# A four-layer graph network on one core: the negative part of layer 1's activation in half-size buffers

## The chip, the cores and the metric

The kernel runs on one core of a Trainium2 chip. The metric is the device time of that core in microseconds. The kernel before takes 2318.61 us, the median of three runs (2318.61 to 2320.24). One further execution was recorded by the hardware profiler; its own time was 2319.3 us, and its span, from the first to the last instruction, is 2317.5 us.

## The reference, cut to what matters

A stack of four graph layers is applied to 32 independent tiles. A tile is `x` (512 tokens of 256 features) with its own 512 x 512 matrix `adj`, all float32. Each layer multiplies by `adj`, by small weight matrices, adds `x` back and normalizes every token (`ln`, a layer norm without weights). Layer 1, where the change lies, has one weight and a leaky activation with slope `alpha`:

```
# layer 0: x = ln(x + relu(((1 + eps) * x + adj @ x) @ W1 + b1) @ W2 + b2)
# layer 1:
h = seq @ W.T + b
h = adj @ h
x = ln(x + where(h > 0, h, alpha * h))
# layer 2: a layer norm first, then x + relu(adj @ h @ W_rel + b_rel + h @ W_root), then ln
# layer 3: epsilon * x + adj @ x, a dense layer of 1024, an rms norm, silu, a dense layer back to 256, ln
```

## The kernel before, in words

**Tiles and layers.** The 512 tokens of a tile lie as 4 chunks of 128 (NC = 4) over the 128 partitions; a half of the tokens is two chunks (HC = 2). `layer0` to `layer3` list the operations of one tile, in a loop over the 32 tiles (`plan.graph` is the tile's number). The products with `adj` and most dense products use seven block products in place of eight (`seven`), which costs VectorE the sums of blocks (`right_sums`, `left_sums`) and the additions that put the products together (`put`).

**Layer 1's end.** For each half of the tokens, `dense_tok` leaves W times the aggregate in PSUM; VectorE writes `v` = b * (row sum) + that, chunk by chunk. Then ScalarE writes `neg` = relu(-v) for the half (`act`, line 1072), VectorE does x = x - alpha * neg (`stt` with `nalpha`, line 1073) and then v = max(v, 0) + x (line 1074). `Norm.half` adds up v on ScalarE. After both halves the tile's `h`, `xx` and, with one `stt` for each chunk, `u` (the bias terms of layer 2) follow.

**An order written by a planner.** None of these calls issues anything. They record operations, and `Plan.order` places all 16956 of them with a list scheduler of its own: each engine in turn takes, of the operations that could start at the earliest moment, the one with the lowest rank. The rank of an operation is its tile's number times 42, plus how much TensorE work of its tile stands before the work that needs it; the last three tiles (LATE = 3) are spaced by the third number of a rule in place of 42. `best` (line 348) works out the order for every rule in `RULES` (line 95) and keeps the one whose last operation starts first by the planner's own table of durations. Of the two rules, that is the first, with 10. The order of the instructions on the engines in the trace is this rule's. The program then issues the operations in that order on five engines; waits between engines are semaphores.

**Rooms.** SBUF buffers are placed by the same planner. There are 36 tiles of 1024 floats for each partition (`rooms`), each made of two halves. A value that covers all tokens (`tok()`, `room()`) takes a whole one; a value of half the size (`short()`) takes a half. A room is taken when the planner places the first operation that uses it, and is free again after the last. `rooms_free` decides whether an operation may take its rooms:

```
if not r.whole and k < len(halves):
    taken[pool, False] = k + 1
    at = max(at, halves[k][0])
    continue
...
n += pool.spare[min(op.graph - oldest, len(pool.spare) - 1)]
if n >= len(whole):
    return None
```

So an operation that takes a whole room must leave a reserve of whole rooms that grows with how far its tile is ahead of the oldest unfinished one: none, 2, 4, and 4 for tiles three and more ahead (`spare` on line 526). An operation that takes a half has no such duty while a half stands free beside an occupied one; only if there is none must it break a whole room under the same reserve. Where both exist, `Pool.take` (line 127) breaks a whole room instead if one has been free for more than 1 us longer than the half. At most five tiles are in work at once (FLIGHT = 5). Halves are otherwise used by the block sums of the dense layers (`dense_sums`, three at a time), by the row sums, and by two values of layer 3.

Of the kernel before, what the change touches and what calls it, by code (L numbers as in the profile page):

```python
# [11 lines left out]
AF = mybir.ActivationFunctionType  # L12
ALU = mybir.AluOpType
# [7 lines left out]
def span(ap):  # L21

    n = 1
    for d in ap.shape[1:]:
        n *= d
    return n
# [65 lines left out]

RULES = [(42, 2, 10, 0.5), (42, 2, 16, 0.5)]


class Pool:
# [122 lines left out]
class Plan:  # L221
# [126 lines left out]
    def best(self):  # L348


        rule = min(RULES, key=lambda rule: self.order(*rule)[0])
        return self.order(*rule)[1]
# [109 lines left out]
def tile_gnn_stack(ctx: ExitStack, tc: tile.TileContext, a: dict, out: bass.AP):  # L462
# [26 lines left out]
    B, N, D = a["x"].shape  # L489
# [6 lines left out]
    HC = NC // 2  # L496
# [36 lines left out]
    def scalar(func, n, x, times=scalar_time, **kw):  # L533
        columns = sum(k in ("scale", "bias") and not isinstance(v, float) for k, v in kw.items())
        return "scalar", "activation", times(n, columns), (x,), dict(func=func, **kw)
# [9 lines left out]
    def act(o, x, func, **kw):  # L545
        plan.do(o, scalar(func, span(o), x, **kw))
# [20 lines left out]
    def stt(o, x, s, y, op0, op1):  # L567
        times = (vector_time if isinstance(s, float) else columns_time)(span(o))
        way = "vector", "scalar_tensor_tensor", times, (x, s, y), dict(op0=op0, op1=op1)
        plan.do(o, way)  # L570
# [11 lines left out]
    def room(*shape):  # L582
        return Part(Room(rooms)).shaped(*shape)

    def short(*shape):
        return Part(Room(rooms, whole=False)).shaped(*shape)

    def small(*shape):
        return Part(Room(smalls)).shaped(*shape)
# [4 lines left out]
    def tok():  # L594
        return room(NC, D)

    def half(t, h):
        return t[:, h * HC : (h + 1) * HC]
# [16 lines left out]
    def constant(name, shape):  # L615
        return const.tile(shape, F32, tag=name, name=name)
# [150 lines left out]
    def aggregate(x, adjacency):  # L767

        aT = room(DC, N)
        blocks = [  # L770
            x[:, j * HC : (j + 1) * HC, k * P : (k + 1) * P] for j in range(2) for k in range(2)
        ]
        t = room(4, HC, P)
        right = right_sums(*blocks, [t[:, i] for i in range(3)], t[:, 3])

        def product(m, ps, first):
            for k in range(HC):
                mm(ps, right[m][:, k, :], adjacency.left[m][:, k, :], first and k == 0, k == HC - 1)

        def block(i, k):  # L780
            return aT[:, k, i * TH : (i + 1) * TH]

        def take(ps, i, k):
            copy(block(i, k), ps)

        def put(ps, i, k, more):
            if more:
                add(block(i, k), ps, block(i, k))
            else:
                take(ps, i, k)  # L790

        seven(*(bank(TH) for _ in range(3)), product, take, put)
        return aT

    def dense_tok(steps, h):

        ps = bank(HC, D)
        for n, (xT, W) in enumerate(steps):
            for i in range(HC):
                c = h * HC + i  # L800
                mm(
                    ps[:, i, :], xT[:, c * P : (c + 1) * P], W,
                    n == 0 and i == 0, n == len(steps) - 1,
                )
        return ps
# [69 lines left out]
    def column_sums(t):  # L875

        few = small(N // Q)
        plan.do(  # L880
            few,
            (
                "vector", "tensor_reduce", vector_time(N), (t.shaped(N // Q, Q),),
                dict(axis=mybir.AxisListType.X, op=ALU.add, apply_transpose=True),
            ),
        )
        for q in range(1, P // Q):
            add(few[0:Q], few[0:Q], few[q * Q : (q + 1) * Q])
        return few[0:Q]

    def by_token(o, sums, *ops):

        for q in range(P // Q):
            ts(o[q * Q : (q + 1) * Q], sums[:, q :: P // Q], *ops)
# [141 lines left out]
    def load_x(b):  # L1036
        x = tok()
        src = a["x"][b].rearrange("(p c) d -> p c d", c=NC)
        if b:
            plan.move(x, src, N * D / 256, late=1.6)  # L1040
        else:
            for h in range(2):
                plan.move(half(x, h), half(src, h), N * D / 512, late=1.6)
        return x

    def layer0(x, adjacency):
        adjacency.sums()
        adjacency.with_loops(loop0)
        aT = aggregate(x, adjacency)
        adjacency.restore()  # L1050
        plus_row(x, b2_0)
        h1 = Wide(FC0)
        dense_feat(aT, A1_0, b1_0, h1, lambda f: act(h1.pair(f), h1.pair(f), AF.Relu))
        norm = Norm(x)
        dense_add(x, dense_sums(h1.rooms[:1], h1.rooms[1:]), A2_0, norm.half)
        norm.scales((1.0, LN_EPS))
        return norm.scaled()

    def layer1(x, adjacency):

        rows = adjacency.row_sums()
        aT = aggregate(x, adjacency)
        rs = small(NC)
        by_token(rs, column_sums(rows), 1.0, None, ALU.mult)
        v, neg = tok(), tok()
        norm = Norm(v)
        for h in range(2):
            ps = dense_tok([(aT[:, k, :], W_1[:, k, :]) for k in range(DC)], h)
            for i in range(HC):
                c = h * HC + i  # L1070
                stt(v[:, c, :], b_1, rs[:, c : c + 1], ps[:, i, :], ALU.mult, ALU.add)
            act(half(neg, h), half(v, h), AF.Relu, scale=-1.0)
            stt(half(x, h), half(neg, h), nalpha, half(x, h), ALU.mult, ALU.add)
            stt(half(v, h), half(v, h), 0.0, half(x, h), ALU.max, ALU.add)
            norm.half(h)

        norm.scales((1.0 + LN_EPS, LN_EPS * LN_EPS), (0.25, 0.25 * LN_EPS))
        h = norm.scaled(0)
        xx = norm.scaled(1)
        u = tok()  # L1080
        for c in range(NC):
            stt(u[:, c, :], shift_rel, rs[:, c : c + 1], shift_2, ALU.mult, ALU.add)
        return h, xx, u
# [68 lines left out]
    x = load_x(0)  # L1152
# [8 lines left out]
    nalpha = constant("nalpha", [P, 1])  # L1161
# [3 lines left out]
    x = layer0(x, adjacency)  # L1165
# [7 lines left out]
    add(shift_2, shift_2, b_2)  # L1173
    A_2 = weight_sums("A_2", *blocks_of(Wroot, Wrel))
    h = layer1(x, adjacency)
    W1_3 = weight("L3_gnn_W1")
    W2_3 = weight("L3_gnn_W2")
# [9 lines left out]
    for b in range(1, B):  # L1187
        plan.graph = b
        x, adjacency = load_x(b), Adjacency(b)
        h = layer1(layer0(x, adjacency), adjacency)  # L1190
        layer3(layer2(*h, adjacency), adjacency, b)
# [44 lines left out]
```

## Time and profile before

| what | value |
|---|---|
| median of three runs | 2318.61 us (2318.61 to 2320.24) |
| profiled execution, its own time | 2319.3 us |
| its span | 2317.5 us |
| TensorE matmul busy | 2295.5 us, 99% |
| TensorE weight load busy | 2089.9 us, 90% |
| VectorE busy | 2120.0 us, 91% |
| ScalarE busy | 1642.6 us, 71% |
| GpSimd busy | 256.9 us, 11% |
| granted TensorE clock | 0.999 |
| DMA, mean share of 16 engines | 19.1% for the data queue |

The span is that of the profiled execution; 1.8 us of its own time lie outside it. A group of the profile gives the engine, the operation, the result and its sources by buffer name, the shapes, the count, the busy time and the mean of one. Line 298 is the planner's `issue` helper, through which every planned operation goes, so groups are told apart by names and shapes: `room` is any of the 36 rooms, `few` the small vectors, `ps` a bank of PSUM.

### The profile page before, as it was taken

How to read it: one execution, taken by the hardware profiler on the slowest of the kernel's cores; microseconds unless marked ns; L12 is line 12 of the kernel's file. 1: busy time of each engine (PE TensorE's matmuls, PEld its weight loads, DVE VectorE, ACT ScalarE, POOL GpSimd, SP SyncE). 2: the span in 40 equal slices, each digit the busy share in tenths (PEclk: the TensorE clock that was granted, in tenths of full speed). 3: DMA queues.
4: the chain of work that ended last, by engine and by line, in shares of the span. 5: the costliest groups of instructions: out<-in, count | busy, mean ns of one | idle time of the engine just before them, and what ended most of it. 6: DMA issues, size and time to landing. Idle time of an engine off the chain costs nothing.

```text
span 2317.5 us, 41158 instructions
## 1 busy us (share of the span) xinstructions
PE 2295.5 (99%) x14002; PEld 2089.9 (90%) x14002; DVE 2120.0 (91%) x5428; ACT 1642.6 (71%) x4444; POOL 256.9 (11%) x167
## 2 busy tenths in 40 slices
PE   9999999999999999999999999999999999999998
PEld 7889899999999999999999999999999999998988
DVE  8989999999899999999999999989999899989897
ACT  4676677776776776777767776767677677676776
POOL 0000001101101101011011111010110101101110
PEclk9999999999999999999999999999999999999999
DMA  7001222112221122211222211222112222201101
GB/s 241 21 18 19 62 58 60 24 55 62 58 60 28 54 59 65 55 43 41 56 65 57 60 25 56 61 58 59 38 46 58 65 55 52 78 13 24 55 15 42
DMA packets 223746, 122.83 MB, mean 53 GB/s; under 512 B 142896, under 2 KB 194352, under 8 KB 223536
## 3 DMA queue, kind: packets, MB, share of 16 engines
q1 hardware_dynamic: 223536, 120.20, 19.1%
q8 instruction: 111, 1.82, 0.3%
q14 instruction: 99, 0.81, 0.1%
HBM read 78.92 MB, written 24.97 MB: 45 GB/s over the span
## 4 chain that ended last, share of the span: by engine, by line
PE 89%; DVE 7%; ACT 2%; DMA 1%; issue 1%; SPq 0%; POOL 0%; ACTq 0%; DVEq 0%
PE ps L298 89%; DVE room L298 6%; ACT room L298 1%; ACT scrap L298 1%; DVE few L298 1%; DMA room<-in_x_dram 1%; DMA L_gnn_W<-in_L_gnn_W_dram 0%; DMA room<-in_adj_dram 0%; DMA L_gnn_b<-in_L_gnn_b_dram 0%; DMA diagonal<-room 0%; SPq L316 0%; ACT L298 0%; DVE A L298 0%; DVE L_gnn_W_root L298 0%; POOL few L298 0%
## 5 line engine op out<-in xcount | busy, mean ns | idle before, releaser
L298 PE MATMUL ps<-room,room 128*128 128x256 f32 x3584 | 930.9, 381 | 5.7 <-DVE room L298 3.2
L298 DVE TENSOR_TENSOR room<-room,room 128x512 f32<-128x512 f32 (+1 forms) x1360 | 773.0, 590 | 5.4 <-ACT room L298 2.8
L298 DVE TENSOR_TENSOR room<-ps,room 128x256 f32<-128x256 f32 (+1 forms) x1344 | 605.6, 469 | 143.7 <-PE ps L298 136.4
L298 PEld LDWEIGHTS ps<-room,room 128*128 128x128 f32 x3584 | 617.3, 191 | 70.3 <-DVE room L298 7.1
L298 PE MATMUL ps<-L_gnn_W,room 128*128 128x128 f32 (+1 forms) x3584 | 544.3, 290 | 1.9 <-DVE room L298 1.0
L298 PEld LDWEIGHTS ps<-L_gnn_W,room 128*128 128x128 f32 x3584 | 505.6, 191 | 33.7 <-ACT room L298 1.9
L298 PEld LDWEIGHTS ps<-A,room 128*128 128x128 f32 x3072 | 460.5, 191 | 47.3 <-DVE room L298 14.1
L298 PE MATMUL ps<-A,room 128*128 128x128 f32 x3072 | 486.9, 276 | 0.9 <-DVE room L298 0.7
L298 POOL TENSOR_TENSOR few<-few,mhalf 128x4 f32<-128x4 f32 (+2 forms) x161 | 256.2, 1598 | 2054.5 <-DVE few L298 1883.1
L298 ACT ACTIVATE room<-room,few 128x256 f32<-128x256 f32 x627 | 335.0, 596 | 159.9 <-DVE few L298 159.7
L298 PE MATMUL ps<-room,L_gnn_W 128*128 128x256 f32 x1536 | 416.4, 380 | 0.6 <-DVE room L298 0.5
L298 ACT ACTIVATE room<-ps,L_gnn_b_c 128x256 f32<-128x256 f32 x768 | 311.0, 476 | 122.3 <-PE ps L298 117.9
L298 DVE TENSOR_TENSOR room<-room 128x256 f32<-128x256 f32 (+1 forms) x640 | 308.7, 492 | 13.9 <-ACT room L298 8.2
L298 PE MATMUL ps<-room,A 128*128 128x256 f32 x1152 | 320.0, 380 | 1.1 <-ACT room L298 0.8
L298 ACT ACTIVATE room<-room 128x1024 f32<-128x1024 f32 (+2 forms) x260 | 240.8, 939 | 87.3 <-DVE room L298 84.4
L298 PEld LDWEIGHTS ps<-room,L_gnn_W 128*128 128x128 f32 x1536 | 274.5, 191 | 30.1 <-DVE room L298 1.9
L298 ACT ACTIVATE room<-ps 128x256 f32<-128x256 f32 (+1 forms) x513 | 180.1, 373 | 153.3 <-PE ps L298 153.1
L298 ACT ACTIVATE scrap<-room,few 128x256 f32<-128x256 f32 x504 | 250.7, 499 | 39.0 <-DVE few L298 38.3
L298 ACT ACTIVATE scrap<-room 128x256 f32<-128x256 f32 x504 | 206.7, 411 | 88.3 <-DVE room L298 79.8
L298 PEld LDWEIGHTS ps<-room,A 128*128 128x128 f32 x1152 | 202.8, 191 | 22.8 <-ACT room L298 2.0
L298 ACT ACTIVATE room<-room,L_gnn_rms_weight_c 128x512 f32<-128x512 f32 x256 | 173.2, 712 | 13.1 <-DVE room L298 11.0
L298 DVE TENSOR_TENSOR room<-room,loop 128x256 f32<-128x256 f32 x256 | 101.1, 411 | 2.9 <-DMA diagonal<-room 1.8
(57 smaller groups left out, 1110.6 us busy)
## 6 DMA issues: line engine op xcount, KB each, us to landing
room<-in_adj_dram SPq DMA_DIRECT2D x128, 256.0 KB, 5.0
room<-in_x_dram SPq DMA_DIRECT2D x31, 512.0 KB, 5.9
out_dram<-room SPq DMA_DIRECT2D x31, 512.0 KB, 3.2
room<-room SPq DMA_DIRECT2D x480, 32.0 KB, 2.0
diagonal<-room SPq DMA_DIRECT2D x62, 128.0 KB, 1.8
room<-in_adj_dram SPq DMA_DIRECT2D x124, 64.0 KB, 1.9
room<-diagonal SPq DMA_DIRECT2D x62, 128.0 KB, 2.2
room<-line SPq DMA_DIRECT2D x30, 256.0 KB, 3.3
```

What stands on the lines that cost most here:

```text
L298: getattr(getattr(self.nc, engine), method)(to, *(put(x) for x in args), **kw)
```

## The change

`neg` is no longer one whole room that holds both halves of the tokens. In each pass of the loop over the halves a half room is asked for with `short(HC, D)`, used by the Relu and by the `stt` with `nalpha`, and given back. Beside it the second rule is taken out of `RULES`. The instructions of the program, their engines, shapes and number are the same.

```diff
-RULES = [(42, 2, 10, 0.5), (42, 2, 16, 0.5)]
+RULES = [(42, 2, 10, 0.5)]
...
-        v, neg = tok(), tok()
+        v = tok()
         norm = Norm(v)
         for h in range(2):
             ps = dense_tok([(aT[:, k, :], W_1[:, k, :]) for k in range(DC)], h)
             for i in range(HC):
                 c = h * HC + i
                 stt(v[:, c, :], b_1, rs[:, c : c + 1], ps[:, i, :], ALU.mult, ALU.add)
-            act(half(neg, h), half(v, h), AF.Relu, scale=-1.0)
-            stt(half(x, h), half(neg, h), nalpha, half(x, h), ALU.mult, ALU.add)
+            neg = short(HC, D)
+            act(neg, half(v, h), AF.Relu, scale=-1.0)
+            stt(half(x, h), neg, nalpha, half(x, h), ALU.mult, ALU.add)
             stt(half(v, h), half(v, h), 0.0, half(x, h), ALU.max, ALU.add)
             norm.half(h)
```

## The prediction

> **What bounds the kernel now.** I read the first part of the page, then the busy time in four stretches, then TensorE's waits, then the groups that the change touches. First the page: busy time, share of the span, instructions.
>
> ```profile
> PE 2295.5 (99%) x14002; PEld 2089.9 (90%) x14002; DVE 2120.0 (91%) x5428; ACT 1642.6 (71%) x4444; POOL 256.9 (11%) x167
> ```
>
> TensorE is the bound, VectorE is not far behind. A mean hides where the slack lies, so next the windows view: stretch, its length, then busy time of PE, PEld, DVE, ACT and POOL, clock, DMA share.
>
> ```profile
> 72.00:290.00 218.00, 213.22 (x1272) 190.78 (x1270) 201.96 (x522) 147.22 (x391) 19.80 (x14) 1.00 0.12 29
> 290.00:1955.00 1665.00, 1665.00 (x10191) 1521.11 (x10190) 1532.03 (x3896) 1207.55 (x3290) 194.14 (x118) 1.00 0.20 52
> 1955.00:2309.00 354.00, 351.13 (x2201) 321.27 (x2199) 318.88 (x814) 248.33 (x660) 37.83 (x25) 1.00 0.14 38
> 2309.00:2317.50 8.50, 0.00 (x0) 0.00 (x0) 2.86 (x13) 4.14 (x11) 1.72 (x3) 0.66 0.47 185
> ```
>
> For 1665 us TensorE never stands still. Its idle time lies at the edges: 5.88 us in the first 72 (the page of windows of 72 us gives 66.12 busy there), 218.00 - 213.22 = 4.78 us up to 290, 354.00 - 351.13 = 2.87 us in the tail, and 8.5 us after the last matmul. Who ends TensorE's waits from 2046 on, and from 55 to 290 (the waits view in each window: total, times, longest)?
>
> ```profile
> PE ps L298 <- DVE room L298: 2.2, 4, 1.1
> PE ps L298 <- ACT room L298: 0.2, 1, 0.2
> ...
> PE ps L298 <- DVE room L298: 3.5, 7, 1.5
> PE ps L298 <- ACT room L298: 1.5, 3, 0.7
> ```
>
> At both edges it is VectorE's results that come late, mostly. What the change touches are two groups (by form: count, busy, mean ns of one, idle before), and one tile's pair of them in the middle, from the timelines of ScalarE and VectorE (start, duration):
>
> ```profile
> L298 ACT ACTIVATE room<-room 128x512 f32<-128x512 f32 x64 | 39.8, 622 | 9.4 <-DVE room L298 7.8
> L298 DVE SCALAR_TENSOR_TENSOR room<-room,nalpha,room 128x512 f32<-128x512 f32 x64 | 47.1, 737 | 0.9 <-ACT room L298 0.9
> ```
>
> ```profile
> 1435.82 0.61 ACT L298 ACTIVATE room<-room 128x512 f32<-128x512 f32 x1
> 1438.09 0.63 ACT L298 ACTIVATE room<-room 128x512 f32<-128x512 f32 x1
> ```
>
> ```profile
> 1436.54 0.73 DVE L298 SCALAR_TENSOR_TENSOR room<-room,nalpha,room 128x512 f32<-128x512 f32 x1
> 1439.26 0.73 DVE L298 SCALAR_TENSOR_TENSOR room<-room,nalpha,room 128x512 f32<-128x512 f32 x1
> ```
>
> Each is 64 instructions, two a tile, already on half the tokens. The whole room of `neg` is held from 1435.82 to 1439.26 + 0.73 = 1439.99: 4.2 us of the 71.2 us that a tile takes (the same Relu stands at 1364.64 one tile before).
>
> **What the Trainium skill says.** "Perfetto Trace Analysis", Identifying the Most-Contended Engine, warns that matmul busy time does not tell how near TensorE is to its limit and asks for the busy share of the weight loads. Here that is 2089.9 / 2317.5 = 90%, and 1521.11 / 1665 = 91% in the middle; together with no wait at all in the middle, I take TensorE as full there. The same page, Optimization Strategy, says that a gap which repeats on the engine that should be full can mean that there is too little SBUF for the next tile. The trace shows no such gap between 290 and 1955, so space is not what limits the middle. "VectorE: DVE Perf Modes", on the TRN2 errata, puts a fixed cost on each instruction; more or larger instructions would thus cost something, but the change alters neither count nor size.
>
> **The change part by part.**
>
> *Instructions.* Removed 0, added 0. The Relu stays 128x512 (622 ns), the `stt` stays 128x512 (737 ns), no DMA moves with them: 64 x 0 = 0 us.
>
> *The second rule.* The plan before is the first rule's, which stays. Taking the other out changes nothing by itself; it only leaves the new plan with no alternative: 0 us.
>
> *The room.* A whole room for 4.2 us becomes a half for about 1.5 us (1435.82 to 1437.27) and a half for 1.9 us (1438.09 to 1439.99). This pays only where an operation waits for a room. I followed the kernel's own bookkeeping of rooms along the trace's order of instructions:
>
> In the middle (tiles 5 to 27) nine whole rooms and a half stand free when the Relu comes, eight whole after it. Nobody waits for a room in those 4.2 us, so nothing moves: 0 us for 23 tiles. If a wait did appear in each, it would be paid in full, since TensorE has no idle time to hide it.
>
> At the start, tile 0's Relu is at 54.45. Between its two halves, at 58.76, a block sum of another tile takes a half and breaks a whole room for it; now it can use the half beside `neg`, and one whole room more stays. The same happens at 160.58 inside tile 2's `neg` (159.19 to 162.52), with five whole rooms free and tile 3 waiting for one: its `u` write needs five and finds four. From there the order can shift until about 290.
>
> In the tail, tile 28's Relu comes at 2046.43 with five whole rooms and one half free. It is two tiles ahead of the oldest, so it must leave four, and takes the fifth. Tiles 29 and 30 wait to write `u`, need five as well, and get their rooms at 2054.06 and 2057.38. With the change `neg` uses the old half, five whole rooms stay, and tile 29's `u` may start some 7.6 us sooner. It is a value that is only needed in layer 2 (whose products begin for tile 29 at 2092.6), so it occupies a room sooner than it is of use. What is late next is not `neg` of the second half itself: tile 28's layer 2 begins on TensorE at 2087.6, about 34 us after the last step of its layer 1 (2053.13). It is the other takers of rooms, all of which come in another order for the last 263 us.
>
> The trace does not show the new order, so I bound its cost. Best: all idle time of the two affected stretches goes, -(4.78 + 2.87) = -7.65 us. Worst: the tail feeds TensorE as poorly as the stretch 72 to 217, where rooms are shortest: 4.31 us idle in 145 (the 72 us windows give 70.82 of 73 and 69.87 of 72), 2.97%. Over 2309 - 2046.4 = 262.6 us that is 7.8 us against 2.55 now (idle from 2046 on: 1.26 + 0.15 + 0.41 + 0.73), +5.25 us; and the start's 4.78 us double: together +10.0 us. I take the middle of -7.65 and +10.0, which is +1.2 us. Sum: 0 + 0 + 0 + 1.2: span 2317.5 to 2318.7, own time 2319.3 to 2320.5. The median of the runs stands 0.7 us below the profiled execution's own time, so 2319.8.
>
> **The rivals.** A difference of 0.2%, 4.6 us, is about what a measurement of this kernel can tell from none.
>
> *Same*, 2319.8 (2314.0 to 2323.2): the middle cannot move, the edges shift by a few us either way. For it: 1665 of 2317.5 us without a wait and with eight rooms to spare. A form of it is that the change does not do what it says for the time: only addresses of rooms differ and the order stays, 2318.6. Against that form: tile 28's Relu releases a taker at once.
>
> *Slower by the tail*, 2323.9: at 2046.43 the room that is saved goes to `u` of tile 29, rooms for the values that TensorE needs come later, and the tail runs at the start's supply: +5.25. It decides from 4.6 us more, that is 7.2 us idle in the last 263. For it: the whole rooms there fall to two, and VectorE, whose results end TensorE's waits, is 90% busy (318.88 of 354). Against: the shift is one room for 7.6 us.
>
> *Slower in the middle*, 2324.7: the weight loads wait 46 times for VectorE between 290 and 1955, 11.9 us in all, 0.26 us each, none of which stops a matmul today. If the new order let one such wait through for each tile, 1665 / 71.2 = 23.4 tiles give 6.1 us. It needs 0.2 us a tile. Against: no room is short there.
>
> *Faster*, 2313.5: two thirds of the 7.65 us go, -5.1, since rooms are what start and tail lack. For it: operations waiting for rooms at both places. Against: the idle time is VectorE's lateness, and its work does not shrink.
>
> **How the numbers follow.** Same 0.54. Slower 0.32: by the tail 0.24, in the middle 0.05, by the start alone 0.03. Faster 0.14. The tail is reordered as a whole with little idle to win and more to lose, hence slower over faster. The likeliest is same, 2319.8. For 8 in 10 the range goes from 2313.0, just below the faster case, to 2329.0, the worst sum (2318.6 + 10.0 = 2328.6); I leave out some 0.05 below and 0.10 above.
>
> **What would show it.** Right: 64 Relus and 64 `stt` with `nalpha` at 622 and 737 ns; TensorE busy for the whole of 290 to 1955; a repeat of 71.2 us; tile 29's `u` (VectorE, from `shift_rel`) between the two halves of tile 28; differences only before 290 and after 1955. Wrong: idle time of TensorE that repeats in the middle, or more than 7.2 us of it after 2046, or the 8.5 us after the last matmul grown, because another tile's end stands beside the last one's.

## The result, and the profile after

The changed kernel takes 2323.11 us (median of 20 runs, 2321.32 to 2325.10) against 2319.34 us of the kernel before in the same comparison (20 runs): ratio 1.0016, 95% interval 1.0009 to 1.0023. That is 3.77 us, or 0.16%: inside the 0.2% that the prediction called the same, inside its range, but at the upper end of the likeliest case (2323.2) and three times the 1.2 us of its sum. The profiled execution of the changed kernel took 2323.66 us with a span of 2321.9 us, 4.4 us more than before by either measure.

The first part of the page of the changed kernel:

```profile
PE 2297.9 (99%) x14002; PEld 2091.5 (90%) x14002; DVE 2119.8 (91%) x5410; ACT 1640.7 (71%) x4443; POOL 256.5 (11%) x167
```

VectorE has 18 instructions fewer than before (5410 for 5428) and ScalarE one fewer, so not every instruction stayed as it was: in its new order the planner sets 53 short pauses on VectorE (`memset` of `pause`, about 0.1 us each) where it was 72, and it gives three operations to the other one of VectorE and ScalarE. The two groups of the change are the same, by form:

```profile
L298 DVE SCALAR_TENSOR_TENSOR room<-room,nalpha,room 128x512 f32<-128x512 f32 x64 | 47.0, 735 | 2.0 <-ACT room L298 2.0
L298 ACT ACTIVATE room<-room 128x512 f32<-128x512 f32 x64 | 39.9, 623 | 9.3 <-DVE room L298 7.6
```

735 and 623 ns where it was 737 and 622: the time is not in these instructions. The windows view (stretch, length, busy time of PE, PEld, DVE, ACT, POOL, clock, DMA share, GB/s) shows the stretch that matters, the middle and the tail, first in the changed kernel:

```profile
150.00:175.00 25.00, 21.71 (x120) 18.84 (x119) 23.94 (x55) 18.40 (x48) 2.64 (x2) 0.93 0.04 12
290.00:1955.00 1665.00, 1664.94 (x10188) 1520.10 (x10188) 1531.22 (x3892) 1205.97 (x3287) 194.24 (x118) 1.00 0.20 52
2046.00:2309.00 263.00, 260.17 (x1635) 238.78 (x1633) 238.20 (x588) 186.79 (x499) 28.34 (x18) 1.00 0.10 24
```

then the first and the last of them in the kernel before:

```profile
150.00:175.00 25.00, 23.38 (x133) 19.97 (x132) 23.88 (x55) 20.73 (x54) 2.64 (x2) 1.00 0.04 12
2046.00:2309.00 263.00, 260.44 (x1645) 238.66 (x1643) 237.57 (x607) 191.60 (x512) 30.45 (x20) 1.00 0.10 26
```

In 25 us TensorE gets through 120 matmul records where it was 133 (a product stands as two records in these traces), with 1.67 us less busy time and a granted clock of 0.93. The middle is as full as it was, and the tail has 2.83 us of idle time against 2.56, far from the 7.2 us that the prediction named as a sign of being wrong. To put a number on each stretch I added up, over all successive products in a trace, the time from one start to the next beyond what a product takes when nothing waits (0.432 us at 256 columns, 0.223 us at 128), and took the time from the last product's end to the end of the span by itself:

| us lost on TensorE | before | after | difference |
|---|---|---|---|
| first product to 150 | 13.35 | 13.29 | -0.06 |
| 150 to 176 | 2.97 | 6.33 | +3.36 |
| 176 to 290 | 1.43 | 1.89 | +0.46 |
| 290 to 1955 | 10.04 | 10.40 | +0.36 |
| 1955 to 2046 | 1.54 | 1.23 | -0.31 |
| 2046 to the last product | 5.47 | 6.59 | +1.12 |
| after the last product | 8.57 | 7.97 | -0.60 |
| sum | 43.37 | 47.70 | +4.33 |

The difference of the sums is that of the two spans (2321.85 - 2317.52). Three quarters of it lie in 26 us. TensorE's timeline there (start, duration, what, idle before and who ended it), kernel before:

```profile
161.46 0.59 PE L298 MATMUL ps<-room,A 128*128 128x256 f32 x2
161.89 1.14 PE L298 MATMUL ps<-room,room 128*128 128x256 f32 x4
162.87 1.05 PE L298 MATMUL ps<-L_gnn_W,room 128*128 128x128 f32 x8
164.41 0.71 PE L298 MATMUL ps<-L_gnn_W,room 128*128 128x128 f32 x4 [0.49 <-DVE room L298]
164.96 1.03 PE L298 MATMUL ps<-room,room 128*128 128x256 f32 x4
```

and after:

```profile
161.39 0.59 PE L298 MATMUL ps<-room,A 128*128 128x256 f32 x2
161.82 1.05 PE L298 MATMUL ps<-L_gnn_W,room 128*128 128x128 f32 x8
162.71 1.03 PE L298 MATMUL ps<-room,A 128*128 128x256 f32 x4
164.35 1.16 PE L298 MATMUL ps<-L_gnn_W,room 128*128 128x128 f32 x8 [0.61 <-DVE room L298]
167.08 1.32 PE L298 MATMUL ps<-L_gnn_W,room 128*128 128x128 f32 x8 [1.57 <-ACT room L298]
168.79 1.12 PE L298 MATMUL ps<-A,room 128*128 128x128 f32 x4 [0.39 <-DVE room L298]
169.71 1.91 PE L298 MATMUL ps<-L_gnn_W,room 128*128 128x128 f32 x8
171.41 1.28 PE L298 MATMUL ps<-room,room 128*128 128x256 f32 x3
```

A product of `room` with `room` here is tile 1's layer-3 aggregate; those of `L_gnn_W` and `A` with `room` at 128 columns are tile 0's last dense layer. Before, the two take turns from 161.89 on, and tile 1 covers the time in which tile 0's operands are prepared. After, tile 1's first product comes at 171.41, 9.5 us later, and tile 0 is left with tile 3's two products for company: waits of 0.61, 1.57 and 0.39 us.

What came ahead of it is on ScalarE. Its timeline before, tile 2's two Relus being the 128x512 lines without `rms_weight`:

```profile
159.19 0.61 ACT L298 ACTIVATE room<-room 128x512 f32<-128x512 f32 x1
159.71 0.71 ACT L298 ACTIVATE room<-room,L_gnn_rms_weight_c 128x512 f32<-128x512 f32 x1
160.32 0.45 ACT L298 ACTIVATE room<-ps,L_gnn_b_c 128x256 f32<-128x256 f32 x1
160.68 0.62 ACT L298 ACTIVATE room<-room 128x512 f32<-128x512 f32 x1
161.20 1.57 ACT L298 ACTIVATE room<-room,few 128x256 f32<-128x256 f32 x3
```

and after:

```profile
159.12 0.61 ACT L298 ACTIVATE room<-room 128x512 f32<-128x512 f32 x1
159.64 0.71 ACT L298 ACTIVATE room<-room,L_gnn_rms_weight_c 128x512 f32<-128x512 f32 x1
160.25 0.81 ACT L298 ACTIVATE room<-ps,L_gnn_b_c 128x256 f32<-128x256 f32 x2
160.96 0.62 ACT L298 ACTIVATE room<-room 128x512 f32<-128x512 f32 x1
161.48 1.08 ACT L298 ACTIVATE room<-room,few 128x256 f32<-128x256 f32 x2
```

The second Relu comes 1.84 us after the first instead of 1.49, because one more activation of tile 3 has gone ahead of it. This is the first place in the whole program where the two orders differ.

The theory that I tested follows from the planner's bookkeeping of rooms and banks along these orders. *Rooms:* at tile 2's first Relu five whole rooms are free, and tile 2 is two ahead of the oldest tile, so it must leave four. A whole room for both halves is asked for once. Half rooms are asked for twice, no half stands free at the second asking, and `rooms_free` then makes an operation wait until the last room of its reserve is free in time, not only the one that it takes. There the last of the five is the very room that the first half has just given back (its reader, the `stt`, runs from 159.76 to 160.52). So the second Relu may not start before that, and ScalarE takes a second activation of tile 3 first (two in the line at 160.25, where there was one). *Banks:* behind the Relu stands tile 1's normalized input (`room<-room,few`), now at 161.48. At 161.82 tile 1's product is not ready, and tile 0 takes the seventh of the eight PSUM banks. Tile 1 is one ahead of the oldest and must leave one bank (`spare` of `banks` is 0, 1, 1), so it may not have the eighth. Before, tile 1 took the seventh at 161.89 and tile 0, the oldest, the eighth.

I call this theory A. Against it stood theory B, that the loss is spread over start and tail or comes from the tail, and theory C, that the waits for a room or a bank are not the cause.

### The profile page after: what moved, and what is told of

Its sections match the earlier page's. It is cut to its first block, busy times and chain, and to the rows that moved or that the text cites. A ratio compares the mean times of both kernels' runs of the same rounds, so it can differ in the third digit from the quotient of the medians.

```text
span 2321.9 us, 41125 instructions
## 1 busy us (share of the span) xinstructions
PE 2297.9 (99%) x14002; PEld 2091.5 (90%) x14002; DVE 2119.8 (91%) x5410; ACT 1640.7 (71%) x4443; POOL 256.5 (11%) x167
## 4 chain that ended last, share of the span: by engine, by line
PE 85%; DVE 11%; ACT 2%; DMA 1%; issue 1%; SPq 0%; ACTq 0%; DVEq 0%
PE ps L298 85%; DVE room L298 10%; DVE few L298 1%; ACT room L298 1%; ACT scrap L298 1%; DMA L_gnn_W<-in_L_gnn_W_dram 0%; DMA room<-diagonal 0%; DMA L_gnn_ln_beta_c<-in_L_gnn_ln_beta_dram 0%; SPq L316 0%; DMA room<-room 0%; DVE pause L1198 0%; ACT L298 0%; DVE A L298 0%; DVE L_gnn_W_root L298 0%; DVE L_gnn_W L298 0%
```

## The experiments

Every run is compared with the kernel before on the same chip in the same comparison. Medians of the kernel before were 2319.51, 2319.56 and 2319.25 us in three such comparisons, and 2319.34 us beside the changed kernel, so a figure "under the changed kernel" holds to some 0.2 us at best.

### Which tiles carry the loss

The first four differ only in which tiles use half rooms:

```diff
+        apart = plan.graph != 2
+        both = None if apart else tok()
...
-            neg = short(HC, D)
+            neg = short(HC, D) if apart else half(both, h)
```

with `apart` as shown for the first, then `plan.graph == 2`, `3 < plan.graph < 28` and `plan.graph > 27`.

> The changed kernel, but tile 2 alone keeps one whole room for both halves. Theory A (nearly all of the loss comes from tile 2: its second Relu must wait for its half, and tile 1 then loses a PSUM bank): the idle time of TensorE between 150 and 175 us returns to that of the kernel before, no half-speed clock there, span 2317.5 to 2319.5 us, some 3 to 4 us under the changed kernel. Theory B (the loss is spread over start and tail, or comes from the tail as the prediction's slower case had it): at most 1.5 us under the changed kernel.

Measured: 2320.39 us, ratio 1.0002 (0.9994 to 1.0011), 2.7 us under the changed kernel. The loss from 150 to 176 is 2.97 us, that of the kernel before. What is left, 0.88 us, is in the tail (6.93 us from 2046 on against 5.47). The gain is a little less than A's 3 to 4 us; the place is A's.

> The kernel before, but tile 2 alone takes half a room for each half. Theory A: the whole loss is there already, span 2320.5 to 2322.5 us, with the wait of TensorE of 1.6 us near 165 us and the half-speed clock behind it. Theory B: within 1 us of the kernel before.

Measured: 2322.81 us, ratio 1.0014 (1.0007 to 1.0020): 3.30 of the 3.77 us from one tile out of 32. Its window and TensorE's waits from 150 to 175 (total, times, longest):

```profile
150.00:175.00 25.00, 21.71 (x128) 18.73 (x127) 23.93 (x56) 19.37 (x51) 2.64 (x2) 1.00 0.04 12
```

```profile
PE ps L298 <- ACT room L298: 2.3, 2, 1.6
PE ps L298 <- DVE room L298: 1.0, 2, 0.6
```

The waits are those of the changed kernel to the tenth. The half-speed clock that I expected behind them is missing: clock 1.00, and 128 records in the stretch instead of 120. This is taken up below.

> Half rooms for tiles 4 to 27 alone, whole ones elsewhere. The prediction's step for the middle (eight whole rooms free, nobody waits): the time of the kernel before within 0.5 us, the same order of instructions, only other rooms. The rival of the middle (a wait in each tile): +6 us.

Measured: 2319.42 us, ratio 0.9998 (0.9990 to 1.0006). Its middle:

```profile
290.00:1955.00 1665.00, 1665.00 (x10190) 1520.62 (x10189) 1532.48 (x3896) 1207.63 (x3289) 194.26 (x118) 1.00 0.20 52
```

The line shows TensorE without a pause, as in the kernel before, for 24 tiles with half rooms. I had expected the same order, and it did not stay: in the planner's list 668 of the 16956 places hold another operation, 108 of TensorE's own among them, and none of it makes TensorE wait.

> Half rooms for tiles 28 to 31 alone. The prediction's slower case (the room saved at tile 28 goes to tile 29's u and starves the tail): +5 us. Theory A: the tail moves the end by no more than -1 to +2 us, though its order differs.

Measured: 2320.57 us, ratio 1.0004 (0.9996 to 1.0012), 1.06 us over the kernel before, with 1.46 us more lost from 2046 on and 0.59 us less after the last product. The 5 us of the prediction's slower case are not there. The interval alone does not tell 1.06 us from nothing; the trace's 1.46 - 0.59 = 0.87 us is the firmer figure, and the changed kernel's trace has 1.12 - 0.60 = 0.52 us. 3.30 and 1.06 add up to 4.36, against the changed kernel's 3.77.

### Room or bank

Three kernels take one wait of theory A away by the planner's rule for it. In the first, one named product may take the bank that is kept in reserve:

```diff
-                    n += pool.spare[min(op.graph - oldest, len(pool.spare) - 1)]
+                    if op is not self.ops[914]:
+                        n += pool.spare[min(op.graph - oldest, len(pool.spare) - 1)]
```

> The changed kernel, but the first product of tile 1's layer-3 aggregate may take a PSUM bank without the reserve of one bank. Theory A (the late Relu costs time because tile 0 then takes the last free bank but one and tile 1 may not take the reserve): TensorE works on tile 1 between 163 and 169 us, its wait of 1.6 us near 165 us goes, 1.5 to 3.5 us under the changed kernel. Theory C (tile 1 is late because its data is late, the bank does not matter): no change.

Measured: 2319.35 us, ratio 0.9999 (0.9991 to 1.0007), 3.8 us under the changed kernel, slightly more than expected. TensorE's timeline:

```profile
163.21 1.05 PE L298 MATMUL ps<-room,room 128*128 128x256 f32 x4
164.10 0.61 PE L298 MATMUL ps<-L_gnn_W,room 128*128 128x128 f32 x4
164.54 1.03 PE L298 MATMUL ps<-room,A 128*128 128x256 f32 x4
165.41 1.05 PE L298 MATMUL ps<-L_gnn_W,room 128*128 128x128 f32 x8
166.32 1.10 PE L298 MATMUL ps<-room,room 128*128 128x256 f32 x4
```

Tile 1 is back among tile 0's products at 163.21, though tile 2's second Relu is still late (1.85 us after the first). One more bank for one product of 6976 takes the loss away: 2.68 us from 150 to 176. Theory C falls for the bank. So the Relu's 0.35 us cost nothing by themselves; they decide who gets a bank.

In the second, the Relu's own wait goes. The new third argument of `Room` marks the second half room of tile 2 as given without the reserve:

```diff
-                    n += pool.spare[min(op.graph - oldest, len(pool.spare) - 1)]
+                    if not r.free:
+                        n += pool.spare[min(op.graph - oldest, len(pool.spare) - 1)]
...
-            neg = short(HC, D)
+            neg = Part(Room(rooms, False, plan.graph == 2 and h == 1)).shaped(HC, D)
```

> The changed kernel, but the second half room of tile 2's negative part is given without the reserve of whole rooms. Theory A: the second Relu of tile 2 starts at 160.6 to 160.7 us as in the kernel before (160.68), tile 1's product follows in its old place, and the loss between 150 and 175 us goes: 2 to 3.5 us under the changed kernel. Theory C (half a room as such shifts the order, waiting or not): the loss stays.

Measured: 2320.94 us, ratio 1.0006 (0.9998 to 1.0015), 2.2 us under the changed kernel, the low end of what A expected. Its Relus stand 1.49 us apart, as before the change, tile 1's first product follows 2.71 us after the first of them (2.70 before), and the loss from 150 to 176 is 2.97 us again. Half a room as such does no harm there; asking again does. The remaining 1.4 us lie in the stretch from 176 to 290 (2.15 us against 1.43) and in the tail.

In the third, an operation waits only for the room or bank that it takes, with the same number in reserve, in every tile:

```diff
-                    at = max(at, whole[n][0])
+                    at = max(at, whole[taken[pool, True] - 1][0])
```

> The changed kernel, but an operation waits until the room that it takes is free, no longer until the last room of its reserve is free; the number of rooms in reserve is the same, for rooms and banks. Theory A: such waits cost time at the start, where the reserve reaches to rooms just given back: the second Relu of tile 2 no longer waits, and the time falls below the kernel before, 2315 to 2319 us. Rival: the reserve's time kept the order good elsewhere, and the time rises, 2321 to 2326 us.

Measured: 2339.13 us, ratio 1.0088 (1.0075 to 1.0102). Theory A's number was wrong by 20 us, and the rival's by 13. The start did become better (0.82 us lost from 176 to 290 against 1.43), but the middle broke:

```profile
290.00:1955.00 1665.00, 1653.82 (x10068) 1505.26 (x10068) 1521.82 (x3835) 1187.15 (x3236) 174.44 (x116) 1.00 0.20 52
```

TensorE is idle for 11.2 us where it was never idle, and by the sum over products the middle loses 31.6 us where it was 10.0. The waits of VectorE in the same stretch:

```profile
DVE room L298 <- PE ps L298: 80.7, 96, 1.8
DVE room L298 <- DMA room<-in_adj_dram: 31.1, 22, 2.3
```

The second line is new: in the kernel before, no wait of VectorE for the loads of `adj` appears in that stretch. About once a tile (1665 / 71.2 = 23.4) VectorE now stands still for a load, 1.4 us each time. That these waits are what TensorE loses was not tested. So waiting for the reserve, which cost 0.35 us at tile 2, can't simply be dropped everywhere. Why the loads come late without it stays open.

### The half-speed clock

In the changed kernel's profile the granted clock is 0.5 for 3.41 us from 168.9 on, 1.9 us after the wait of 1.57 us ended and right behind that of 0.39 us. The eight records (four products) at 169.71 need 1.91 us where eight of the same form at 164.35 need 1.16. To see what that is worth, seven products with zeros that leave the sum as it is were put into the wait, and `pause` was cleared once at the start:

```diff
+    nc.vector.memset(pause, 0.0)
...
             op.ways[op.way][1]()
+            if op is plan.ops[522]:
+                ps = op.out.place()[:, 0:48]
+                for _ in range(7):
+                    nc.tensor.matmul(ps, ident, pause, start=False, stop=False, skip_group_check=True)
```

> The changed kernel with seven products more on TensorE (128 weights by 48 columns of zeros, added to a sum that they leave as it is), issued in its wait near 165 us, plus one memset at the start. If part of the loss is the half-speed clock that followed that wait in the profile of the changed kernel (3.4 us at half speed, 8 products at 0.43 instead of 0.22 us, 1.4 to 1.7 us): no half-speed stretch near 169 us, and 0.7 to 1.7 us under the changed kernel. If the wait alone counts: no change, or up to 0.5 us over it.

Measured: 2322.38 us, ratio 1.0013 (1.0006 to 1.0019), by the medians 0.7 us under the changed kernel, while the two intervals overlap for the most part. TensorE's timeline with the filler:

```profile
165.73 0.94 PE L299 MATMUL ps<-L_gnn_W,room 128*128 128x128 f32 x6 [0.61 <-DVE room L299]
166.50 1.66 PE L1205 MATMUL ps<-pause,ident 128*128 128x48 f32 x14
168.00 0.34 PE L299 MATMUL ps<-L_gnn_W,room 128*128 128x128 f32 x1
```

The wait is filled, and no half-speed stretch follows. But the profile of the kernel with tile 2 alone had the unfilled wait and no such stretch either. The mean granted clock of every execution, on record to three digits, says more. A half-speed stretch of 3.41 us takes 0.07% off it (3.41 / 2 / 2321.9). It is 0.998 in 9 of 20 executions of the changed kernel and in 13 of 21 of the kernel with tile 2 alone, and 0.999 in the others; with the filler it is 0.998 in 1 of 19, with the one bank or with tile 2 whole in none of 13, in the kernel before in 1 of 49, 1 of 39 and 1 of 41. The counts can be low (one profile with such a stretch, that of the last kernel below, still reads 0.999). So the slow clock comes in some executions only, and mostly goes when the wait is filled or gone.

Its share of the 3.77 us is not settled. In the changed kernel the median is 2322.96 us at 0.998 and 2323.23 at 0.999; with tile 2 alone it is 2322.95 and 2321.62. The 2321.62 still stands 2.1 us above the kernel before, so as far as these clocks tell, the larger part of tile 2's loss does not need the slow clock. In the one profile that has it, the stretch from 150 to 176 lost 6.33 us, against 4.90 with tile 2 alone, where the order up to there is the same: 1.43 us in that execution.

### The tail, and the rule taken out

Two kernels ask which tile of the tail matters (`apart` is `plan.graph in (29, 30)`, then `plan.graph == 28`), one runs the kernel before with the other rule, and one puts together what was learned (`apart` is `plan.graph < 28`, with the one bank of above):

```diff
-RULES = [(42, 2, 10, 0.5), (42, 2, 16, 0.5)]
+RULES = [(42, 2, 16, 0.5)]
```

> The kernel before, but half rooms for tiles 29 and 30 alone. If the tail's loss of 1.06 us comes from these two: 2320.2 to 2320.9 us. If it comes from tile 28, as the prediction had it: 2319.5 us, as before.

Measured: 2320.22 us, ratio 1.0003 (0.9995 to 1.0011), 0.97 us over the kernel before. Lost from 2046 on: 6.90 us, as with all four tiles (6.93). Again the interval alone does not tell this from nothing, and the trace carries the reading.

> The kernel before, but half rooms for tile 28 alone. The prediction's tail mechanism (the room that tile 28 saves is taken sooner by another tile): 1 us or more over the kernel before. If tile 28 does not matter: within 0.4 us of it, tile 29's u where it was (2054.06 us).

Measured: 2318.81 us, ratio 0.9997 (0.9989 to 1.0005). Four operations of 16956 stand in another place, 5.47 us are lost from 2046 on, and tile 29's `u` starts at 2054.39 in a trace that runs some 0.3 us later from its start. Tile 28 does not matter.

> The kernel before with the second rule alone, the one that the change takes out (last three tiles spaced by 16). The prediction says that taking it out costs nothing because the first rule's order was in use: this rule alone should be no faster than the kernel before; a tail in another order with more idle time: 2 to 8 us over it.

Measured: 2324.42 us, ratio 1.0021 (1.0013 to 1.0030), 5.2 us over the kernel before. This tail loses 12.15 us from 2046 on, a half-speed stretch of the clock among them. The rule that was taken out was the worse one for the kernel before.

> Half rooms for tiles 0 to 27, whole ones for 28 to 31, and the first product of tile 1's layer-3 aggregate may take a PSUM bank of the reserve. If the losses of start and tail are separate and add up: the start as with the one bank alone (2319.35 us), less the tail's 1.06: 2318.0 to 2319.0 us, at or a little under the kernel before. If they do not add up: 2319.3 us or more.

Measured: 2318.50 us, ratio 0.9998 (0.9989 to 1.0006). That fits two losses that add up, as expected: 4.6 us under the changed kernel. Against the kernel before, 0.75 us by the medians cannot be told from nothing, so this is no version that beats both.

## Why the prediction was right, and where it was not

**Instructions: right for the change's two groups.** 64 and 64, 623 and 735 ns. "Removed 0, added 0" does not hold for the whole program: 19 pauses fewer, and three operations on another engine, since the planner decides both with the order.

**The second rule: right.** The first rule's order was in use, and alone the other costs 5.2 us. Worked through for the changed kernel, `best` keeps the first rule of the two as well, so no better plan was lost with it.

**The middle: right in time.** Zero, by the run with tiles 4 to 27 alone (0.9998) and by 1664.94 of 1665 us busy. "Nothing moves" was too much: operations changed places there, and TensorE did not wait for it.

**Tile 0 at 54.45: place wrong, cost right.** Nothing moved before 160 us (-0.06 us up to 150).

**Tile 2: the place was right, the mechanism was not.** The prediction named 159.19 to 162.52 as a place where the order can shift, with five whole rooms free and four to leave. But its step "the room" said that the change "pays only where an operation waits for a room" and counted only rooms that come free for others; PSUM banks do not appear in it at all. The step left out that a buffer that is given back and asked for again must pass the reserve again. That second asking is the new wait at tile 2. It is worth 0.35 us on ScalarE and, by way of the bank, 3.30 us of time (the run with tile 2 alone). The prediction had bounded the start's loss at +4.78 us, so the size fits its bound; its weight did not: "by the start alone" had 0.03.

**The tail: mechanism wrong, size smaller.** "Tile 29's `u` may start some 7.6 us sooner" did not happen: in the changed kernel it starts at 2057.87, 7.63 us after tile 28's Relu at 2050.24, exactly the old distance. By the bookkeeping of the run with the tail alone, the room that `neg` leaves went to a copy of tile 27's aggregate within 2 us. The tail's cost came from tiles 29 and 30, 0.97 us, not from tile 28 (2318.81 us alone). The prediction's kind of shift, a saved room that goes to another tile sooner, is there at tile 29: by the planner's list of the run with these two tiles a block sum of tile 30 starts 2.7 us sooner and a transfer of tile 28 1.1 us. How that leads to the cost was not followed further.

**The sum.** +1.2 was the middle between bounds; measured was +3.77, within them (-7.65 to +10.0). The mis-sized term is the start: up to 290 the profile lost 3.76 us more (-0.06 + 3.36 + 0.46). That the total stayed under 4.6 us, and so the same, is in part luck: most of it came by a wait and a bank that the prediction did not have, and nothing in its sum held them to that size.

**What the prediction could have read.** It says that the trace does not show the new order, and bounds its cost. But `Plan.order` works the new order out from the kernel's text alone, and returns when the last operation starts by the planner's table of durations. Against the kernel before, this start is later by 3.98 us in the changed kernel (measured 3.77), by 2.94 with tile 2 alone (3.30), by 0 with the middle alone (-0.09), by 1.03 with the tail alone (1.06) and with tiles 29 and 30 (0.97), by 0.66 with the one bank (-0.21), by 1.56 without the reserve (1.38), and by 6.72 with the other rule (5.17). The table knows no clock, so this too speaks for the order as the larger part of the loss. For the kernel that waits only for what it takes, the table says 1.97 us sooner where the chip took 19.6 us more: what broke there is not in the table.

**Rivals.** The tail's 5 us, the middle's 6 us and the faster case did not occur. That the order stays wholly as it was is refuted as well.

## What to carry to other kernels

A smaller buffer with a shorter life is not free where buffers are rationed by a reserve: each time it is asked for, it passes the rationing again, and one asking for a large buffer can be the cheaper one. In a greedy order a delay is priced by the decision that it turns, not by its length: 0.35 us on an engine with slack decided who got a PSUM bank, and that was worth 3.3 us. Where TensorE was full and buffers were to spare, 24 such changes cost nothing, so the edges of the program, where buffers are short, deserve the first look. And where a program makes its own order before it runs, that order can be had before any run: work it out for the changed text, and then ask which effects its table of durations leaves out.

## What the runs showed of the hardware that was not expected

In the changed kernel's profile three waits of TensorE within some 5 us (0.61, 1.57 and 0.39 us) came ahead of a fall of the granted clock to 0.5 for 3413 ns, in which 128-column products took about 0.43 us from start to start instead of 0.22. Two other profiles, of the last two kernels above, have one half-speed stretch each of the same 3413 ns, one from 2084.2 us with the other rule and one from 11.1 us with bank and tail together. The profile with tile 2 alone had the same waits without it, and the clocks on record show 0.998 in 9 of 20 and 13 of 21 executions of the two kernels with these waits, in 1 of 19 where the longest is filled. So waits of this length lead to it in some executions and not in others; what decides between them was not tried.
